# delta*u*B of every second state built tokens first and turned by TensorE into PSUM for the scan of a selective state-space layer

## The chip, the cores and the metric

The kernel runs on one core of one Trainium2 chip. Its time is the device time of one execution in microseconds. Five engines work side by side, each through its own instruction queue in order: TensorE (PE, with its weight loads PEld), VectorE (DVE), ScalarE (ACT), GpSimd (POOL) and SyncE (SP, which here only issues DMAs). SBUF is the working memory with 128 partitions; PSUM is the memory that TensorE writes into.

## What is computed

An image batch x of shape (4, 128, 128, 128), rows, columns, channels last, goes through two residual layers, each on a group-normalised input:

```
x = x + deformable_conv(group_norm(x))       # layer 0: offsets, bilinear samples, depthwise 3x3, pointwise
x = x + mamba2(group_norm(x))                # layer 1: every image row is a sequence of 128 tokens
```

Layer 1 is two blocks, one after the other, of this form (256 inner channels d, 16 states n, all fp32):

```
u, res = split(h @ in_w);  u = silu(causal_conv4(u) + cb)
dt, Bm, Cm = split(u @ xw);  delta = softplus(dt @ dtw + dtb);  A = -exp(A_log)
for t in tokens:                             # per channel d and state n
    s[d,n] = exp(delta[t,d]*A[d,n]) * s[d,n] + delta[t,d]*u[t,d]*Bm[t,n]
    y[t,d] = sum_n s[d,n] * Cm[t,n]
h = ((y + u*D) * silu(res)) @ out_w
```

## The kernel before

Layer 1 works on groups of `SR` = 4 image rows, so on `TB` = 512 tokens; the 256 channels are `NC` = 2 halves of 128 partitions. A job is one group in one of the two blocks (`NL` = 2): 4 images x 32 groups x 2 = 256 jobs. Their order is group 0 block 0, group 1 block 0, group 0 block 1, group 1 block 1, then the next pair of groups. `layer1` calls `pre` of the next job and then `main` of this one.

`pre` (L484) makes what the scan needs: four-tap convolution by 4 matmuls per channel half into a PSUM tile `pu`, Silu on ACT (L508), the gate `g` (`pr`, L513 to L518), the projection `pdb` and its copy `dbl` (L521, L524), B and C sent to DRAM as `bcd` (L526), then `pdt` and the softplus for each half: Abs, Exp, plus one, Ln on ACT (L538 to L546), two VectorE instructions for each half (L547, L548), and `de` (delta) and `du` (delta times u) for both halves (L549, L550). A job of block 0 starts from a load of layer 0's result; a job of block 1 needs the output of the same group in block 0.

`main` (L553) opens a PSUM tile `y` of two banks with u*D (L561) and then runs 8 steps q, each with `NQ` = 2 states. A step loads the rows of B and of C for its states from `bcd`, broadcast to all partitions (L570); ACT clears the first token of each row in `da` (L575, so that a scan starts anew there) and writes exp(delta*A) into the rest (L580, one instruction per half and state); VectorE multiplies `du` by B into `hs` for each state (L586), scans all 2048 numbers per partition in one instruction (L592), and multiplies the result by C (L596); TensorE transposes the 16 pieces of 128 x 128 and adds them up in `y` (L604, shown under the helper's line L128), which sums over the states and turns to tokens first. Behind the last step VectorE multiplies `y` by the gate (L607), TensorE turns the product back (`pyg`, L612), ACT copies it (`yg`, L613), TensorE applies the output projection (`pout`, L617 or L624 and L626) and ACT copies the result out (L619 or L630).

Layer 0 of image 0 runs alone. Then layer 0 of image b+1 is interleaved with layer 1 of image b, and layer 1 of the last image runs alone. Layer 0 works in units: GpSimd issues 8 gathers for a unit (L364), VectorE weighs the samples (`gw`, L382, two products of 1024), TensorE transposes and adds them into `p4` (helper line L128), ACT copies `p4` out (L396), and TensorE sums the 3 x 3 convolution into `acc` (L415).

The instructions are written in program order; a scheduler then sets the order on each engine, and tiles of one pool and tag take turns in its `bufs` buffers: a new tile waits until the last reader of the tile that had its buffer is done. The PSUM buffers of 512 fp32 numbers per partition are shared out like this: pool `ps`, tag "t", 2 (all of layer 0 but `acc`), `psa` 2 (`acc`), `ps1`, tag "t", 2 (`pu`, `pr`, `pdb`, `pdt`, `pyg`, `pout`), `psy` 2 (`y`).

Of the kernel before, what the change touches and what calls it, by code (L numbers as in the profile page):

```python
# [17 lines left out]
P = 128  # L18
# [45 lines left out]
def block_kernel(ctx: ExitStack, tc: tile.TileContext, a: dict, out: bass.AP):  # L64
# [24 lines left out]
    cw = ctx.enter_context(tc.tile_pool(name="w", bufs=1))  # L89
    small = ctx.enter_context(tc.tile_pool(name="small", bufs=1))  # L90
    pb = ctx.enter_context(tc.tile_pool(name="l0b", bufs=1))
    ps = ctx.enter_context(tc.tile_pool(name="l0ps", bufs=2, space=PSUM))
    psa = ctx.enter_context(tc.tile_pool(name="l0psa", bufs=2, space=PSUM))
    p2 = ctx.enter_context(tc.tile_pool(name="l1p2", bufs=1))
    pd = ctx.enter_context(tc.tile_pool(name="l1d", bufs=3, space=DRAM))
    ps1 = ctx.enter_context(tc.tile_pool(name="l1ps", bufs=2, space=PSUM))
    psy = ctx.enter_context(tc.tile_pool(name="l1psy", bufs=1, space=PSUM))

    def loadw(name, shape, src=None, pool=cw, tag=None):
# [33 lines left out]


    dw = loadw("dw", [P, NT, NT], pool=p2, tag="dbl")
    dwb = loadw("dwb", [P, NT], pool=p2, tag="ot")
    pw = loadw("pw", [P, NT, CG], pool=p2, tag="u")
    pwb = loadw("pwb", [P, 1], pool=p2, tag="w1")
    nc.vector.tensor_tensor(
# [15 lines left out]
    alog = loadw("alog", [P, NL, NC, NS], pool=p2, tag="dbl")  # L155
    nc.scalar.activation(aneg, alog, AF.Exp)
    nc.vector.tensor_scalar(aneg, aneg, -1.0, None, ALU.mult)
    dpar = loadw("dpar", [P, NL, NC], pool=p2, tag="ot")
# [4 lines left out]
    cvw = loadw("cvw", [P, NL, DCONV, NC * P], pool=p2, tag="hs")  # L163
    for l in range(NL):
        nc.vector.tensor_tensor(
            inc[:, l], cvw[:, l], inw[:, l].unsqueeze(1).to_broadcast([P, DCONV, NC * P]), ALU.mult
        )


# [312 lines left out]
    def pre(st, l):  # L484

        blk = st["blk"]
        nm = f"{blk}_{l}"
        if l == 0:
            x1t = load_x1(blk, nm)
            st["h"] = next_h()  # L490
            scale, bias = gn2[blk * SR // H]
            nc.scalar.activation(
                st["h"][:, :, DCONV - 1 :], x1t.rearrange("p (s t) -> p s t", s=SR),
                AF.Identity, scale=scale, bias=bias,
            )
        h = st["h"]
        u = p2.tile([P, NC, TB], F32, tag="u", name=f"u_{nm}")
        for c in range(NC):
            px = ps1.tile([P, TB], F32, tag="t", name=f"pu_{nm}_{c}")
            for j in range(DCONV):  # L500
                nc.tensor.matmul(  # L501
                    px.rearrange("p (s t) -> p s t", s=SR),
                    inc[:, l, j, c * P : (c + 1) * P],
                    h[:, :, j : j + P],
                    start=(j == 0),
                    stop=(j == DCONV - 1),
                )
            nc.scalar.activation(u[:, c], px, AF.Silu, bias=cvb[:, l, c : c + 1])  # L508
        g = p2.tile([P, SR, NC * P], F32, tag="g", name=f"g_{nm}", bufs=2)
        for i in range(SR // 2):  # L510
            px = ps1.tile([P, 2, NC * P], F32, tag="t", name=f"pr_{nm}_{i}")
            for j in range(2):
                nc.tensor.matmul(  # L513
                    px[:, j], h[:, 2 * i + j, DCONV - 1 :], resw[:, l, :],
                    start=(j == 0), stop=True, skip_group_check=True,
                )

            tc.keep_in_program_order(nc.scalar.activation(g[:, 2 * i : 2 * i + 2], px, AF.Silu))  # L518
        pdb = ps1.tile([P, TB], F32, tag="t", name=f"pdb_{nm}")
        for c in range(NC):  # L520
            nc.tensor.matmul(pdb[0:XP], xpw[:, l, c, :], u[:, c], start=(c == 0), stop=(c == NC - 1))  # L521

        dbl = p2.tile([XP, TB], F32, tag="dbl", name=f"dbl_{nm}")
        nc.scalar.activation(dbl, pdb[0:XP], AF.Identity, bias=xpb)  # L524
        bcd = pd.tile([2 * NS, TB], F32, tag="bcd", name=f"bcd_{nm}")
        nc.sync.dma_start(bcd, dbl[DTR + 1 : XP, :])  # L526


        de = p2.tile([P, NC, TB], F32, tag="de", name=f"de_{nm}", bufs=2)
        du = p2.tile([P, NC, TB], F32, tag="du", name=f"du_{nm}", bufs=2)  # L530
        es, pdts = [], []
        for c in range(NC):
            pdt = ps1.tile([P, TB], F32, tag="t", name=f"pdt_{nm}_{c}")
            nc.tensor.matmul(
                pdt, dtw[:, l, c * P : (c + 1) * P], dbl[0 : DTR + 1, :], start=True, stop=True
            )
            e = p2.tile([P, TB], F32, tag="e", name=f"e_{nm}_{c}", bufs=2)
            nc.scalar.activation(e, pdt, AF.Abs)  # L538
            nc.scalar.activation(e, e, AF.Exp, scale=-1.0)
            es.append(e)  # L540
            pdts.append(pdt)
        for c in range(NC):
            e = es[c]
            w1 = p2.tile([P, TB], F32, tag="w1", name=f"w1_{nm}_{c}")
            nc.scalar.activation(w1, e, AF.Identity, bias=1.0)
            nc.scalar.activation(du[:, c], w1, AF.Ln)  # L546
# [3 lines left out]
        nc.vector.tensor_tensor(du, de, u, ALU.mult)  # L550
        st.update(u=u, g=g, delta=de, du=du, bcd=bcd)

    def main(st, l):  # L553

        blk = st["blk"]
        nm = f"{blk}_{l}"

        y = psy.tile([P, SR, NC, P], F32, tag="y", name=f"y_{nm}")
        for i in range(SR):
            for c in range(NC):  # L560
                nc.tensor.matmul(  # L561
                    y[:, i, c], st["u"][:, c, i * P : (i + 1) * P], ddiag[:, l, c, :],
                    start=(i % 2 == 0 and c == 0), stop=False, skip_group_check=True,
                )
        for q in range(NS // NQ):
            bc = []
            for w in range(2):
                t = p2.tile([P, NQ, TB], F32, tag=f"bc{w}", name=f"bc{w}_{nm}_{q}", bufs=2)
                n0 = w * NS + q * NQ
                nc.sync.dma_start(t, st["bcd"][n0 : n0 + NQ, :].partition_broadcast(P))  # L570
                bc.append(t)
            da = das[n_da[0] % NDA]
            n_da[0] += 1

            nc.scalar.copy(da.rearrange("p c n s t -> p (c n s) t")[:, :, 0], zero)  # L575
            for c in range(NC):
                dv = st["delta"][:, c].rearrange("p (s t) -> p s t", s=SR)
                for n in range(NQ):
                    s = q * NQ + n
                    nc.scalar.activation(  # L580
                        da[:, c, n, :, 1:], dv[:, :, 1:], AF.Exp, scale=aneg[:, l, c, s : s + 1]
                    )
            hs = p2.tile([P, NC, NQ, TB], F32, tag="hs", name=f"hs_{nm}_{q}")

            for n in range(NQ):
                nc.vector.scalar_tensor_tensor(  # L586
                    hs[:, :, n, :], st["du"], ones[:, 0:1],
                    bc[0][:, n].unsqueeze(1).to_broadcast([P, NC, TB]),
                    op0=ALU.mult, op1=ALU.mult,
                )  # L590
            df = da.rearrange("p c n s t -> p (c n s t)")
            nc.vector.tensor_tensor_scan(  # L592
                df, df, hs.rearrange("p c n t -> p (c n t)"), zero[:, 0:1], ALU.mult, ALU.add
            )
            dc = da.rearrange("p c n s t -> p c (n s t)")
            nc.vector.scalar_tensor_tensor(  # L596
                dc, dc, ones[:, 0:1],
                bc[1].rearrange("p n t -> p (n t)").unsqueeze(1).to_broadcast([P, NC, NQ * TB]),
                op0=ALU.mult, op1=ALU.mult,
            )  # L600
            for c in range(NC):
                for n in range(NQ):
# [145 lines left out]
```

## Time and profile before

| | |
|---|---|
| median of 3 runs | 26672.16 us (26664.46 to 26679.19) |
| the profiled execution | 26698.06 us, of which its span 26696.0 us |
| layer 0 of image 0 alone | 0 to about 3400 us |
| layer 1 of images 0 to 2 beside layer 0 of images 1 to 3 | about 3400 to 21356 us |
| layer 1 of image 3 alone | about 21356 us to the end |

Busy time of the engines in two of these stages, in us and as a share:

| stretch | PE | DVE | ACT | POOL | granted PE clock |
|---|---|---|---|---|---|
| 3400 to 21350 us | 14338 (80%) | 17483 (97%) | 8669 (48%) | 13634 (76%) | 0.89 |
| 21350 us to the end | 2794 (52%) | 5065 (95%) | 2695 (50%) | 0 | 0.69 |

In the lines that follow, a group is a source line, its engine and operation, output<-inputs, their shapes and the count, then the busy time and the mean of one instruction in ns, then the idle time of the engine just before and what ended it. In a timeline a row is the start in us, the duration in us of the row's instructions, engine, line and operation. The strings of 40 digits give a share in tenths for each fortieth of the span.

### The profile page before, as it was taken

The page shows a single profiled execution, that of the slowest core. Times are in us where ns is not written, and L with a number is a line of the kernel's source. Part 1 is how long each engine was busy: PE and PEld are TensorE (multiplying, and loading weights), DVE is VectorE, ACT ScalarE, POOL GpSimd, SP SyncE. Part 2 cuts the span into 40 slices and gives each one's busy share as a digit, 9 for nine tenths or more (in the row PEclk, how much of TensorE's full clock was granted, in tenths as well). Part 3 has the DMA queues.
Part 4 walks back from the last instruction along what each step waited for, and adds up shares of the span by engine and source line. Part 5 has one row for each costly group of instructions (what it writes and reads, how often), then busy time and mean ns, then how long its engine had stood idle before and what let it go on. Part 6 is the DMA issues. An engine that isn't in the chain of part 4 may idle for free. (4 is left out here: it accounts for less than half of the span.)

```text
span 26696.0 us, 294801 instructions
## 1 busy us (share of the span) xinstructions
PE 19620.5 (73%) x112196; PEld 13523.4 (51%) x112196; DVE 23505.8 (88%) x14042; ACT 11605.1 (43%) x18181; POOL 16017.0 (60%) x9222
## 2 busy tenths in 40 slices
PE   4777788878888778887888778888888655555555
PEld 3444455555555555555555555555555443434344
DVE  2232289999999999999999999999999999999999
ACT  0000044444444544444444454444445455555554
POOL 4777777878877767888878667877878400000000
PEclk7888888888999888888998888899998866666666
DMA  5363344456544444455544444444444333333332
GB/s 146 114 172 107 106 147 155 157 170 183 165 153 154 149 144 155 158 173 181 164 154 153 148 143 151 156 150 152 154 154 156 130 107 106 107 106 107 107 106 102
DMA packets 1994602, 3804.53 MB, mean 143 GB/s; under 512 B 771796, under 2 KB 1116116, under 8 KB 1993053
## 3 DMA queue, kind: packets, MB, share of 16 engines
q1 hardware_dynamic: 1550812, 2577.13, 29.9%
q0 software_dynamic: 442368, 1208.55, 14.4%
q8 instruction: 880, 14.42, 0.2%
q14 instruction: 542, 4.43, 0.0%
HBM read 3567.63 MB, written 217.05 MB: 142 GB/s over the span
## 5 line engine op out<-in xcount | busy, mean ns | idle before, releaser
L364 POOL DMA_INDIRECT gt<-table,idx x9216 | 16016.3, 1738 | 5031.5 <-issue 2999.5
L592 DVE TENSOR_TENSOR_SCAN da<-da,zero,hs 128x2048 f32<-128x2048 f32 x2048 | 9176.1, 4481 | 351.7 <-ACT da L580 247.1
L128 PE MATMUL y<-ident,da 128*128 128x128 f32 x32768 | 5252.0, 326 | 3956.1 <-DVE da L596 3955.4
L580 ACT ACTIVATE da<-de,aneg 128x508 f32<-128x508 f32 x8192 | 5550.5, 712 | 5605.2 <-PE y L128 5351.0
L128 PEld LDWEIGHTS y<-ident,da 128*128 128x128 f32 x32768 | 4682.4, 171 | 4953.3 <-DVE da L596 2520.6
L415 PE MATMUL acc<-s,wc 128*64 128x256 f32 (+3 forms) x38400 | 6403.2, 453 | 761.4 <-ACT s L396 760.9
L586 DVE SCALAR_TENSOR_TENSOR hs<-du,ones,bc 128x1024 f32<-128x1024 f32 x4096 | 5093.2, 1277 | 0.0
L415 PEld LDWEIGHTS acc<-s,wc 128*64 128x64 f32 x38400 | 3352.0, 145 | 3083.2 <-issue 1446.2
L596 DVE SCALAR_TENSOR_TENSOR da<-da,ones,bc 128x2048 f32<-128x2048 f32 x2048 | 4807.9, 2348 | 25.9
L382 DVE TENSOR_TENSOR gw<-gt,wt 128x1024 f32<-128x1024 f32 x2304 | 2786.4, 1213 | 2133.3 <-DMA gt<-table,idx 1500.9
L128 PE MATMUL p<-ident,gw 128*128 128x128 f32 x18432 | 2724.3, 299 | 1714.1 <-DVE gw L382 1706.7
L128 PEld LDWEIGHTS p<-ident,gw 128*128 128x128 f32 x18432 | 2292.8, 154 | 2329.3 <-DVE gw L382 1752.7
L396 ACT COPY s<-p 128x512 f32<-128x512 f32 x1152 | 668.6, 581 | 3989.8 <-PE p L128 3982.0
L501 PE MATMUL pu<-hp,inc 128*128 128x512 f32 x4096 | 1808.3, 593 | 0.0
L580 ACT ACT_TABLE_LOAD x1016 | 1303.5, 1283 | 16.8 <-PE y L128 5.7
L501 PEld LDWEIGHTS pu<-hp,inc 128*128 128x128 f32 x4096 | 751.2, 188 | 865.9 <-issue 865.2
L508 ACT ACTIVATE u<-pu,w_cvb 128x512 f32<-128x512 f32 x512 | 324.6, 684 | 1468.9 <-PE y L561 1461.4
L561 PEld LDWEIGHTS y<-ddiag,u 128*128 128x128 f32 x4096 | 579.5, 200 | 192.0 <-issue 192.0
L612 PE MATMUL pyg<-ident,g 128*128 128x128 f32 x2048 | 353.9, 328 | 425.7 <-DVE g L607 424.8
L546 ACT ACT_TABLE_LOAD x500 | 641.5, 1283 | 8.9
L561 PE MATMUL y<-ddiag,u 128*128 128x128 f32 x4096 | 612.1, 284 | 0.0
L263 PE MATMUL pof<-xn,w_offw 128*64 128x512 f32 x2304 | 585.0, 613 | 20.0 <-ACT xn L257 12.0
(118 smaller groups left out, 11036.3 us busy)
## 6 DMA issues: line engine op xcount, KB each, us to landing
bc<-bcd SPq DMA_DIRECT2D x4096, 512.0 KB
gt<-table,idx POOLq DMA_INDIRECT x9216
table<-xt SPq DMA_DIRECT2D x984, 128.0 KB
xt<-in_x SPq DMA_DIRECT2D x124, 320.0 KB
xr<-in_x SPq DMA_DIRECT2D x128, 256.0 KB
x<-xo SPq DMA_DIRECT2D x128, 256.0 KB
x1t<-x SPq DMA_DIRECT2D x128, 256.0 KB
x1t_o<-x SPq DMA_DIRECT2D x128, 256.0 KB
```

The costliest lines, as they stand in the source:

```text
L128: nc.tensor.matmul(o, v, ident, is_transpose=True, start=start, stop=stop, skip_group_check=True)
L364: nc.gpsimd.indirect_dma_start(out=gt[:, v, r], out_offset=None, in_=flat, in_offset=bass.IndirectOffsetOnAxis(ap=idx[:, ri, o : o + 1], a ...
L382: nc.vector.tensor_tensor(gw.rearrange("p r s v c -> p (r s) v c"), gts[h].rearrange("p v r (s c) -> p (r s) v c", c=CG), wv.unsqueeze(3). ...
L396: nc.scalar.copy(st[:, :, 1 : W + 1], p4)
L415: nc.tensor.matmul(accs[b, j + i0][CG * g : CG * g + CG, q : q + rb - ra, :], wc[sl, v, e, :], st[p + 4 * g if p < 4 else 8][sl, ra:rb, kx ...
L501: nc.tensor.matmul(px.rearrange("p (s t) -> p s t", s=SR), inc[:, l, j, c * P : (c + 1) * P], h[:, :, j : j + P], start=(j == 0), stop=(j ...
L546: nc.scalar.activation(du[:, c], w1, AF.Ln)
L561: nc.tensor.matmul(y[:, i, c], st["u"][:, c, i * P : (i + 1) * P], ddiag[:, l, c, :], start=(i % 2 == 0 and c == 0), stop=False, skip_grou ...
L580: nc.scalar.activation(da[:, c, n, :, 1:], dv[:, :, 1:], AF.Exp, scale=aneg[:, l, c, s : s + 1])
L586: nc.vector.scalar_tensor_tensor(hs[:, :, n, :], st["du"], ones[:, 0:1], bc[0][:, n].unsqueeze(1).to_broadcast([P, NC, TB]), op0=ALU.mult, ...
L592: nc.vector.tensor_tensor_scan(df, df, hs.rearrange("p c n t -> p (c n t)"), zero[:, 0:1], ALU.mult, ALU.add)
L596: nc.vector.scalar_tensor_tensor(dc, dc, ones[:, 0:1], bc[1].rearrange("p n t -> p (n t)").unsqueeze(1).to_broadcast([P, NC, NQ * TB]), op ...
```

## The change

In every step q the first state goes on as before: VectorE multiplies `du` by a broadcast row of B, but GpSimd does so in the last image. The product of the second state is made tokens first: at the start of `main`, `du` is transposed by TensorE in two pieces (`pdu`) and copied by ACT into `dut`; in each step ACT scales the four rows' pieces of `dut` by a column of B (`bt`, which `pre` now makes by transposing `dbl`), and 8 transposes turn the result into two PSUM tiles `px`, which the scan reads as its second operand. The scan of 2048 becomes one of 1024 for the first state and two of 512 for the second; it writes to `hs` and not over `da`, whose first column of each row is cleared once at the start. The product with C is one instruction per state. Of B one row is broadcast per step and not two. To make room in PSUM, tag "t" of `ps` and of `ps1` have one buffer each, and `psx` has two.

```diff
-    ps = ctx.enter_context(tc.tile_pool(name="l0ps", bufs=2, space=PSUM))
+    ps = ctx.enter_context(tc.tile_pool(name="l0ps", bufs=1, space=PSUM))
...
-    ps1 = ctx.enter_context(tc.tile_pool(name="l1ps", bufs=2, space=PSUM))
+    ps1 = ctx.enter_context(tc.tile_pool(name="l1ps", bufs=1, space=PSUM))
+    psx = ctx.enter_context(tc.tile_pool(name="l1psx", bufs=2, space=PSUM))
...
-    NDA = 3
-    das = [cw.tile([P, NC, NQ, SR, P], F32, name=f"da{i}") for i in range(NDA)]
-    zero = cw.tile([P, NC * NQ * SR], F32, name="zero")
-    nc.vector.memset(zero, 0.0)
+    NDA = 4
+    das = [cw.tile([P, NC, SR, P], F32, name=f"da{i}") for i in range(NDA)]
+    for t in das:
+        nc.vector.memset(t, 0.0)
...
+        pbt = ps1.tile([P, SR, XP], F32, tag="t", name=f"pbt_{nm}")
+        for i in range(SR):
+            nc.tensor.transpose(pbt[:, i, :], dbl[:, i * P : (i + 1) * P], ident[0:XP, 0:XP])
+        bt = p2.tile([P, SR, NS], F32, tag="bt", name=f"bt_{nm}", bufs=2)
+        nc.scalar.copy(bt, pbt[:, :, DTR + 1 : DTR + 1 + NS])
...
+        dut = p2.tile([P, SR, NC * P], F32, tag="dut", name=f"dut_{nm}")
+        for k in range(SR // 2):
+            pt = ps1.tile([P, 2, NC, P], F32, tag="t", name=f"pdu_{nm}_{k}")
+            for i in range(2):
+                for c in range(NC):
+                    o = (2 * k + i) * P
+                    nc.tensor.transpose(pt[:, i, c, :], st["du"][:, c, o : o + P], ident)
+            nc.scalar.copy(dut[:, 2 * k : 2 * k + 2], pt.rearrange("p s c d -> p s (c d)"))
         for q in range(NS // NQ):
-            bc = []
-            for w in range(2):
...
-            nc.scalar.copy(da.rearrange("p c n s t -> p (c n s) t")[:, :, 0], zero)
...
+            bs = p2.tile([P, TB], F32, tag="bs", name=f"bs_{nm}_{q}", bufs=2)
+            nc.sync.dma_start(bs, st["bcd"][q * NQ : q * NQ + 1, :].partition_broadcast(P))
+            cs = p2.tile([P, NQ, TB], F32, tag="cs", name=f"cs_{nm}_{q}", bufs=2)
+            nc.sync.dma_start(cs, st["bcd"][NS + q * NQ : NS + q * NQ + NQ, :].partition_broadcast(P))
+            hs = [p2.tile([P, NC, TB], F32, tag="hs", name=f"hs_{nm}_{q}_{n}", bufs=4) for n in range(NQ)]
...
+            bv = bs.unsqueeze(1).to_broadcast([P, NC, TB])
+            if last:
+                nc.gpsimd.tensor_tensor(hs[0], st["du"], bv, ALU.mult)
+            else:
+                nc.vector.scalar_tensor_tensor(hs[0], st["du"], ones[:, 0:1], bv, op0=ALU.mult, op1=ALU.mult)
+            h0 = hs[0].rearrange("p c t -> p (c t)")
+            nc.vector.tensor_tensor_scan(
+                h0, da[0].rearrange("p c s t -> p (c s t)"), h0, 0.0, ALU.mult, ALU.add
+            )
+            s = q * NQ + 1
+            xs = [p2.tile([P, 2, NC * P], F32, tag="xs", name=f"xs_{nm}_{q}_{k}", bufs=2) for k in range(SR // 2)]
+            for i in range(SR):
+                nc.scalar.activation(xs[i // 2][:, i % 2], dut[:, i], AF.Copy, scale=st["bt"][:, i, s : s + 1])
             for c in range(NC):
...
+                px = psx.tile([P, SR, P], F32, tag="x", name=f"px_{nm}_{q}_{c}")
+                for i in range(SR):
+                    nc.tensor.transpose(px[:, i, :], xs[i // 2][:, i % 2, c * P : (c + 1) * P], ident)
+                nc.vector.tensor_tensor_scan(
+                    hs[1][:, c], da[1][:, c].rearrange("p s t -> p (s t)"), px.rearrange("p s t -> p (s t)"),
+                    0.0, ALU.mult, ALU.add,
+                )
             for n in range(NQ):
                 nc.vector.scalar_tensor_tensor(
-                    hs[:, :, n, :], st["du"], ones[:, 0:1],
-                    bc[0][:, n].unsqueeze(1).to_broadcast([P, NC, TB]),
+                    hs[n], hs[n], ones[:, 0:1], cs[:, n].unsqueeze(1).to_broadcast([P, NC, TB]),
                     op0=ALU.mult, op1=ALU.mult,
                 )
-            df = da.rearrange("p c n s t -> p (c n s t)")
-            nc.vector.tensor_tensor_scan(
-                df, df, hs.rearrange("p c n t -> p (c n t)"), zero[:, 0:1], ALU.mult, ALU.add
-            )
...
```

The rest of the diff moves set-up tiles to other tags (the convolution weights come in two loads and not one) and lets the transposes into `y` read `hs`.

More of the change, by code (lines that the diff above doesn't have):

```diff
@@ L135, in block_kernel @@
     dw = loadw("dw", [P, NT, NT], pool=p2, tag="dbl")
-    dwb = loadw("dwb", [P, NT], pool=p2, tag="ot")
+    dwb = loadw("dwb", [P, NT], pool=p2, tag="yg")
     pw = loadw("pw", [P, NT, CG], pool=p2, tag="u")
@@ L157, in block_kernel @@
     nc.vector.tensor_scalar(aneg, aneg, -1.0, None, ALU.mult)
-    dpar = loadw("dpar", [P, NL, NC], pool=p2, tag="ot")
+    dpar = loadw("dpar", [P, NL, NC], pool=p2, tag="u")
     for l in range(NL):
@@ L162, in block_kernel @@
     inw = loadw("inw", [P, NL, NC * P], a["inw"][:, :, 0 : NC * P], pool=p2, tag="yg")
-    cvw = loadw("cvw", [P, NL, DCONV, NC * P], pool=p2, tag="hs")
     for l in range(NL):
+        cvw = p2.tile([P, DCONV, NC * P], F32, tag="hs", name=f"w_cvw_{l}", bufs=4)
+        nc.sync.dma_start(cvw, a["cvw"][:, l])
         nc.vector.tensor_tensor(
-            inc[:, l], cvw[:, l], inw[:, l].unsqueeze(1).to_broadcast([P, DCONV, NC * P]), ALU.mult
+            inc[:, l], cvw, inw[:, l].unsqueeze(1).to_broadcast([P, DCONV, NC * P]), ALU.mult
         )
@@ L550, in pre @@
         nc.vector.tensor_tensor(du, de, u, ALU.mult)
-        st.update(u=u, g=g, delta=de, du=du, bcd=bcd)
+        pbt = ps1.tile([P, SR, XP], F32, tag="t", name=f"pbt_{nm}")
[3 more added lines that the diff above has]
+        nc.scalar.copy(bt, pbt[:, :, DTR + 1 : DTR + 1 + NS])
+        st.update(u=u, g=g, delta=de, du=du, bcd=bcd, bt=bt)
     def main(st, l):
         blk = st["blk"]
+        last = blk * SR // H == B - 1
         nm = f"{blk}_{l}"
@@ L564, in main @@
                 )
-        for q in range(NS // NQ):
-            bc = []
-            for w in range(2):
[L568 to L573, printed above, removed]
-            nc.scalar.copy(da.rearrange("p c n s t -> p (c n s) t")[:, :, 0], zero)
-            for c in range(NC):
[L577 to L581, printed above, removed]
-                    )
-            hs = p2.tile([P, NC, NQ, TB], F32, tag="hs", name=f"hs_{nm}_{q}")
+        dut = p2.tile([P, SR, NC * P], F32, tag="dut", name=f"dut_{nm}")
@@ new lines, in main @@
+        for k in range(SR // 2):
[5 more added lines that the diff above has]
+            nc.scalar.copy(dut[:, 2 * k : 2 * k + 2], pt.rearrange("p s c d -> p s (c d)"))
+        for q in range(NS // NQ):
+            bs = p2.tile([P, TB], F32, tag="bs", name=f"bs_{nm}_{q}", bufs=2)
[3 more added lines that the diff above has]
+            hs = [p2.tile([P, NC, TB], F32, tag="hs", name=f"hs_{nm}_{q}_{n}", bufs=4) for n in range(NQ)]
+            da = []
+            for n in range(NQ):
+                d = das[n_da[0] % NDA]
+                n_da[0] += 1
+                s = q * NQ + n
+                for c in range(NC):
+                    dv = st["delta"][:, c].rearrange("p (s t) -> p s t", s=SR)
+                    nc.scalar.activation(d[:, c, :, 1:], dv[:, :, 1:], AF.Exp, scale=aneg[:, l, c, s : s + 1])
+                da.append(d)
+            bv = bs.unsqueeze(1).to_broadcast([P, NC, TB])
[11 more added lines that the diff above has]
+                nc.scalar.activation(xs[i // 2][:, i % 2], dut[:, i], AF.Copy, scale=st["bt"][:, i, s : s + 1])
+            for c in range(NC):
+                px = psx.tile([P, SR, P], F32, tag="x", name=f"px_{nm}_{q}_{c}")
[5 more added lines that the diff above has]
+                )
@@ L585, in main @@
             for n in range(NQ):
                 nc.vector.scalar_tensor_tensor(
-                    hs[:, :, n, :], st["du"], ones[:, 0:1],
-                    bc[0][:, n].unsqueeze(1).to_broadcast([P, NC, TB]),
+                    hs[n], hs[n], ones[:, 0:1], cs[:, n].unsqueeze(1).to_broadcast([P, NC, TB]),
                     op0=ALU.mult, op1=ALU.mult,
                 )
-            df = da.rearrange("p c n s t -> p (c n s t)")
-            nc.vector.tensor_tensor_scan(
-                df, df, hs.rearrange("p c n t -> p (c n t)"), zero[:, 0:1], ALU.mult, ALU.add
-            )
@@ L595, in main @@
[L595 to L602, printed above, removed]
+                for c in range(NC):
                     for i in range(SR):
-                        add_transposed(y[:, i, c], da[:, c, n, i, :], False, q == NS // NQ - 1 and n == NQ - 1)
+                        add_transposed(
+                            y[:, i, c], hs[n][:, c, i * P : (i + 1) * P], False,
+                            q == NS // NQ - 1 and n == NQ - 1,
+                        )
@@ L628, in main @@
                     )
-            ot = p2.tile([P, SR, P], F32, tag="ot", name=f"ot_{nm}")
+            ot = p2.tile([P, SR, P], F32, tag="w1", name=f"ot_{nm}")
             nc.scalar.copy(ot.rearrange("p r c -> p (r c)"), po)
```

## The prediction

> **What bounds the kernel now.** I read the page's engine shares and 40 slices first, then the costliest groups, then busy time by stretch, then the timeline of one period and of one block boundary in the last image.
>
> ```profile
> span 26696.0 us, 294801 instructions
> PE 19620.5 (73%) x112196; PEld 13523.4 (51%) x112196; DVE 23505.8 (88%) x14042; ACT 11605.1 (43%) x18181; POOL 16017.0 (60%) x9222
> DVE  2232289999999999999999999999999999999999
> PEclk7888888888999888888998888899998866666666
> ```
> VectorE is full from the sixth slice on; only the first stage (layer 0 of image 0 alone, to 3400 us) leaves it room. A second less of its work is a second less of time, so long as its queue never stops.
>
> ```profile
> L592 DVE TENSOR_TENSOR_SCAN da<-da,zero,hs 128x2048 f32<-128x2048 f32 x2048 | 9176.1, 4481 | 351.7 <-ACT da L580 247.1
> L586 DVE SCALAR_TENSOR_TENSOR hs<-du,ones,bc 128x1024 f32<-128x1024 f32 x4096 | 5093.2, 1277 | 0.0
> L596 DVE SCALAR_TENSOR_TENSOR da<-da,ones,bc 128x2048 f32<-128x2048 f32 x2048 | 4807.9, 2348 | 25.9
> ```
> One step q is two of L586, one L592, one L596: 2 x 1.277 + 4.481 + 2.348 = 9.383 us. Next, one period of the last image and the boundary behind it (start, duration):
>
> ```profile
> 23008.29 2.48 DVE L586 SCALAR_TENSOR_TENSOR hs<-du,ones,bc 128x1024 f32<-128x1024 f32 x2
> 23010.90 4.48 DVE L592 TENSOR_TENSOR_SCAN da<-da,zero,hs 128x2048 f32<-128x2048 f32 x1
> 23015.42 2.35 DVE L596 SCALAR_TENSOR_TENSOR da<-da,ones,bc 128x2048 f32<-128x2048 f32 x1
> 23017.69 2.48 DVE L586 SCALAR_TENSOR_TENSOR hs<-du,ones,bc 128x1024 f32<-128x1024 f32 x2
> ...
> 23032.17 7.03 PE L501 MATMUL pu<-hp,inc 128*128 128x512 f32 x16
> 23042.46 1.89 PE L513 MATMUL pr<-w_resw,hp 128*128 128x256 f32 x8
> 23048.18 1.91 PE L521 MATMUL pdb<-u,w_xpw 128*41 128x512 f32 x4
> 23050.87 1.98 PE L534 MATMUL pdt<-dbl,w_dtw 9*128 9x512 f32 x4
> 23054.82 1.28 ACT L546 ACT_TABLE_LOAD   x1
> 23069.03 1.20 DVE L550 TENSOR_TENSOR du<-de,u 128x1024 f32<-128x1024 f32 x1
> ```
> The period is 9.40 us, the sum of the durations: nothing is between. `pre` of a later job runs from pu (23032) to du (23069) while VectorE goes on with steps of `main`, which need nothing from it. So a chain of over 35 us at every one of the 256 boundaries is hidden today. By the L607 rows image 0's blocks start near 3400 and the last image's near 21356: a block (8 steps) lasts 17956/192 = 93.5 us beside layer 0 and (26696 - 21356)/64 = 83.4 us in the last image.
>
> **The change, part by part.**
>
> VectorE's work. The scan is cut into one of 1024 from SBUF and two of 512 whose second operand lies in PSUM. L586 and L596 give 1.046 ns per element and 0.206 us fixed; a scan that keeps such a fixed part takes 2.35 us for 1024 and 1.28 us for 512 (2.24 and 1.12 if all of it scaled). PSUM as source: L548 reads it and takes 0.682, L547 the same size from SBUF 0.678, so nothing. No row has a scan with one SBUF input; the far lower bound is L548's rate, 0.68. I take 1.28, since two SBUF inputs do not halve L586's rate, so the slow pace is the scan's own. The C product becomes two of 1.277. A step costs 1.277 + 2.35 + 2 x 1.28 + 2 x 1.277 = 8.74 us, and 7.46 in the last image, where the B product goes to GpSimd. Gain: 0.64 x 8 = 5.1 us per block, 15.4 in the last image.
>
> Added in a step, beside VectorE: ACT gets 4 scaled copies of 256, 0.41 (L243, 260 elements) to 0.48 us (on the line from L343's 0.366 for 128 to L580's 0.712 for 508); I take 0.5. With four L580 it has 4 x 0.71 + 4 x 0.50 = 4.9 us of 7.46. PE gets 8 transposes; 16 of them took 3.65 us in the slow clock of the last image, so 24 take 5.5 us of 7.46. The built program puts step q's copies and transposes ahead of step q-1's products, so inside a block both stay hidden. The L575 copies go, and the broadcasts fall from four rows to three: both off the path. SP's queue issues these loads one step ahead, as before, and POOL's queue holds nothing but the product in the last image. Set-up edits happen once.
>
> GpSimd's product has no row: between VectorE's product of 1.21 us (L549) and GpSimd's own dearest group, 1.74 us (L364), it fits in a 7.46 us step. If it held up VectorE for its whole length it would cost up to 512 x 1.74 = 0.89 ms. L586 takes 1.277 us while GpSimd gathers and 1.279 in the last image without, so I take 0 and keep 0.89 as the other end.
> [...]
>
> The boundary. Both tag-"t" pools fall from two banks to one, and the new transposes of du (pdu) and of dbl (pbt) use the bank of `pre`. The built program's PE order at a boundary of the last image, buffer numbers cut:
>
> ```
> pyg_126_0  y(ddiag)  pout_126_0  pu_126_1_0  pu_126_1_1  pr  pr  pdb_126_1
> pdt_126_1_0  pdt_126_1_1  pbt_126_1  pdu_127_0_0  pdu_127_0_1  px_127_0_0
> ```
> So job 127_0's first px, which VectorE's first PSUM scan waits for, stands behind the whole `pre` of 126_1, and this behind 126_0's output. What is queued behind that scan on VectorE: all the rest of the block. ACT's order is the same, and with one bank each product waits for the copy-out of the last. The chain C from the end of L607 (g):
> - pyg, yg: 1.15 (24110.10 to 24111.25) + 0.59, now twice in a row, then pout 3.62 (24112.29, L617) and its copy 0.59, hand-overs 0.1 each: 7.9.
> - pu: half of 7.03 + Silu 0.68 + 0.1, twice: 8.6. pr: half of 1.89 + 0.60 + 0.1, twice: 3.3. pdb 1.91 + dbl 0.68 + 0.1: 2.7.
> - first pdt 1.15 to its Abs (23050.87 to 23052.02), Abs 0.60, table 1.28, Exp 0.62, L545 0.62, then L547 + L548 on VectorE, 1.36, before the bank is free: 5.7. Before, both pdt stood side by side. Second: 4.3 to L545, then 1.4 on VectorE and 0.7 for pbt: 6.4. bt: 0.3 (between L575's 0.21 and L343's 0.37).
> - pdu 1.15, dut 0.59, two scaled copies 1.0, dut 0.59, two copies 1.0, px 0.5 and hand-overs: 5.0.
> C = 7.9 + 8.6 + 3.3 + 2.7 + 5.7 + 6.4 + 0.3 + 5.0 = 39.9, say 40 us; beside layer 0 ACT also copies two s tiles (0.58 each) and VectorE one statistics group (0.69) inside it: 42.
>
> A block, from g to g, is C, then what VectorE still has to do: two PSUM scans 2.56, C product 1.28, seven steps, the next block's head, g 1.21. Last image: 2.56 + 1.28 + 7 x 7.46 + 2.35 + 1.21 = 59.6, + 40 = 99.6 us, 16.2 more than 83.4. Beside layer 0: 2.56 + 1.28 + 7 x 8.74 + 1.28 + 1.21 = 67.5; layer 0 has 93.5 - 75.1 - 6.35 (L547 to L550, L607) = 12 us of VectorE per block, of which the built order puts seven or eight products of 1.21 inside the chain, so 2 remain: 67.5 + 2 + 42 = 111.5, 18.0 more than 93.5.
> The first stage, with one bank for p, loses nothing to 0.2 ms (a 0.58 us copy for each of 288 units of 11.8 us); I take 0.
> **Sum**: 26.70 + 192 x 0.0180 + 64 x 0.0162 = 26.70 + 3.46 + 1.04 = **31.2 ms**. The profiled run took 26698 us, 26 over the median of 26672; that is nothing here.
>
> **Rivals.**
> 1. *The chain is hidden after all, and the gain stays*: 192 x 5.1 + 64 x 15.4 = 1.96 ms, 24.7 ms, faster. For it: before, `pre` was hidden. It decides where C falls below what a block saves and covers: the added 4.50 ms over 256 blocks is 17.6 us, so C under 24. The rows that are ACT's and VectorE's alone (17 us) and pu (7.03) reach that without any other matmul. 5%, of which 1 near no change.
> 2. *GpSimd's product blocks VectorE* in the last image: up to 31.2 + 0.89 = 32.1 ms. [...] 23%.
> 3. *The chain is longer*: PE goes cold in its gaps (the page grants 0.6 in the last image) and pu, pr, pdb, pdt double, +12.8 us; half of that, 6.4 x 256 = 1.6 ms, gives 32.8. For it: gaps of several us at pdt; against it: pu ran at full pace behind pout. 14%.
> 4. *The chain is shorter*: warm transposes and pout and hand-overs at nothing take off 5 us, 1.3 ms: 29.9; faster PSUM scans would go the same way, and both together reach 29. 8%.
>
> **How the numbers follow.** The likeliest has 50%, its own range 30.4 to 32.0 (C by 3 us). The range 29.5 to 32.9 takes in rivals 2 to 4 nearly whole. Under 0.2% (53 us) would not be told from no change: 1%, faster 4%, slower 95%.
>
> **What would show it.** VectorE idle some 20 us per block beside layer 0 and 30 us in the last image, waiting for px; its busy time near 21.5 ms; scans of 2.35 and 1.28; exp and ln tables loaded twice each per block. Wrong would be: no idle time before the first px scan of a block, or a chain from g to it under 24 us.

## The result and the profile after

The changed kernel takes 31183.35 us (median of 4 runs, 31163.41 to 31192.35), beside 26675.67 us for the kernel before in the same comparison: 1.169 times as long, interval 1.167 to 1.171. The forecast was 31200 us, slower. The profiled execution took 31184.21 us, its span 31182.4.

First the page of the kernel after, its engine shares and VectorE's 40 slices, and then groups (busy us, mean ns of one | idle us just before, and what ended it):

```profile
PE 23808.8 (76%) x131652; PEld 16026.7 (51%) x131652; DVE 20847.6 (67%) x17629; ACT 14695.9 (47%) x24611; POOL 12320.8 (40%) x9734
...
DVE  2322577777777777777777777777777766666666
...
L384 DVE TENSOR_TENSOR gw<-gt,wt 128x1024 f32<-128x1024 f32 x2304 | 2782.9, 1220 | 4376.1 <-PE p L129 2421.8
...
L620 DVE TENSOR_TENSOR_SCAN hs<-da,px 128x512 f32<-128x512 f32 x4096 | 4841.4, 1201 | 703.4 <-PE px L619 703.4
L625 DVE SCALAR_TENSOR_TENSOR hs<-hs,ones,cs 128x1024 f32<-128x1024 f32 x4096 | 5097.1, 1279 | 0.2
L608 DVE TENSOR_TENSOR_SCAN hs<-da,hs 128x1024 f32<-128x1024 f32 x2048 | 4659.4, 2275 | 1.0
...
L604 POOL TENSOR_TENSOR hs<-du,bs 128x1024 f32<-128x1024 f32 x512 | 1821.1, 3557 | 4668.6 <-PE y L129 4273.2
...
L549 DVE SCALAR_TENSOR_TENSOR e<-w,e 128x512 f32<-128x512 f32 x512 | 356.6, 696 | 4408.8 <-ACT w L547 4408.7
```
VectorE has 2.7 ms less work than before (20.85 against 23.51 ms), and yet it was 88% busy and is 67%. It waits before the softplus (L549, 4.4 ms) and before layer 0's products (L384, 4.4 ms, of which 2.05 ms come ahead of the first g, where the kernel before has 1.99), and hardly before the scan out of PSUM (L620, 0.7 ms). The group that carries the idle time is only the first in VectorE's queue behind the gap; what is late has to be looked for in the timeline. One boundary of the last image, of the kernel after (start, duration; in brackets the idle time before and what ended it):

```profile
28043.53 1.23 DVE L637 TENSOR_TENSOR g<-y,g 128x1024 f32<-128x1024 f32 x1 [0.37 <-PE y L129]
28044.67 1.72 DVE L625 SCALAR_TENSOR_TENSOR hs<-hs,ones,cs 128x1024 f32<-128x1024 f32 x1
...
28052.48 3.70 PE L503 MATMUL pu<-hp,inc 128*128 128x512 f32 x8
28057.03 3.70 PE L503 MATMUL pu<-hp,inc 128*128 128x512 f32 x8 [0.63 <-ACT u L510]
28065.15 1.91 PE L523 MATMUL pdb<-u,w_xpw 128*41 128x512 f32 x4 [0.69 <-ACT g L520]
28067.83 1.12 PE L536 MATMUL pdt<-dbl,w_dtw 9*128 9x512 f32 x2 [0.77 <-ACT dbl L526]
28072.22 0.69 DVE L549 SCALAR_TENSOR_TENSOR e<-w,e 128x512 f32<-128x512 f32 x1 [25.82 <-ACT w L547]
28073.69 2.07 PE L536 MATMUL pdt<-dbl,w_dtw 9*128 9x512 f32 x2 [4.74 <-DVE de L550]
28079.03 0.69 DVE L549 SCALAR_TENSOR_TENSOR e<-w,e 128x512 f32<-128x512 f32 x1 [5.39 <-ACT w L547]
28081.45 1.11 PE L582 MATMUL pdu<-ident,du 128*128 128x128 f32 x4 [0.30 <-ACT bt L558]
28084.15 1.06 PE L619 MATMUL px<-ident,xs 128*128 128x128 f32 x4
28086.51 2.33 DVE L620 TENSOR_TENSOR_SCAN hs<-da,px 128x512 f32<-128x512 f32 x2 [3.06 <-PE px L619]
```
g ends at 28044.76, the scan out of PSUM starts at 28086.51: 41.75 us. Between them lie this block's output (7.7 us up to pu), the whole `pre` of the next job, one product behind the other through one bank, then du's transposes, and only then px. The first wait in VectorE's queue, 25.82 us, is booked to L549, because the scheduler put `pre`'s two softplus instructions ahead of the scan. The second, 5.39 us, is the second pdt, which had to wait for the bank; the third, 3.06 us, is px itself.

From the starts of L637 (L607 before) in the two timelines, the period of a block:

| | before | after | difference | times blocks |
|---|---|---|---|---|
| start of the first g | 3570.1 | 3555.8 | -14.3 us | |
| beside layer 0, us per block | 93.12 | 112.69 | +19.57 | x 191 = +3.74 ms |
| last image, us per block | 83.28 | 95.11 | +11.83 | x 64 = +0.76 ms |

The sum is 4.48 ms of the 4.51 ms lost. A block lost 19.6 us beside layer 0, where 18.0 were forecast, and 11.8 in the last image, where 16.2 were.

### The profile page after: what moved, and what is told of

The parts are those of the page before. It is cut to its first block, busy times and chain, and to the rows that moved or that the text cites. A ratio compares the mean times of both kernels' runs of the same rounds, so it can differ in the third digit from the quotient of the medians.

```text
span 31182.4 us, 348664 instructions
## 1 busy us (share of the span) xinstructions
PE 23808.8 (76%) x131652; PEld 16026.7 (51%) x131652; DVE 20847.6 (67%) x17629; ACT 14695.9 (47%) x24611; POOL 12320.8 (40%) x9734
## 4 chain that ended last, share of the span: by engine, by line
DVE 29%; issue 28%; PE 23%; POOL 13%; ACT 4%; DMA 2%; SPq 0%; DVEq 0%; POOLq 0%; ACTq 0%
POOL gt L366 13%; DVE hs L608 9%; DVE hs L620 8%; DVE hs L625 6%; PE acc L417 6%; PE pu L503 4%; DVE hs L606 3%; PE p L129 2%; DMA gt<-table,idx 2%; PE y L129 2%; PE pdt L536 1%; PE pr L515 1%; PE y L571 1%; PE pdb L523 1%; PE px L619 1%
## 5 line engine op out<-in xcount | busy, mean ns | idle before, releaser
L366 POOL DMA_INDIRECT gt<-table,idx x9216 | 10499.0, 1139 | 14166.6 <-DVE gw L384 11167.8
L598 ACT ACTIVATE da<-de,aneg 128x508 f32<-128x508 f32 x8192 | 5455.6, 711 | 6460.0 <-DVE hs L608 3723.5
L129 PE MATMUL y<-ident,hs 128*128 128x128 f32 x32768 | 5821.8, 345 | 1595.3 <-DVE hs L625 1538.8
L129 PEld LDWEIGHTS y<-ident,hs 128*128 128x128 f32 x32768 | 5054.0, 181 | 2655.0 <-DVE hs L625 2299.9
L384 DVE TENSOR_TENSOR gw<-gt,wt 128x1024 f32<-128x1024 f32 x2304 | 2782.9, 1220 | 4376.1 <-PE p L129 2421.8
L619 PE MATMUL px<-ident,xs 128*128 128x128 f32 x16384 | 3167.2, 325 | 3060.4 <-DVE hs L620 2992.4
L620 DVE TENSOR_TENSOR_SCAN hs<-da,px 128x512 f32<-128x512 f32 x4096 | 4841.4, 1201 | 703.4 <-PE px L619 703.4
L625 DVE SCALAR_TENSOR_TENSOR hs<-hs,ones,cs 128x1024 f32<-128x1024 f32 x4096 | 5097.1, 1279 | 0.2
L608 DVE TENSOR_TENSOR_SCAN hs<-da,hs 128x1024 f32<-128x1024 f32 x2048 | 4659.4, 2275 | 1.0
L619 PEld LDWEIGHTS px<-ident,xs 128*128 128x128 f32 x16384 | 2096.6, 163 | 4390.0 <-DVE hs L620 2438.7
L615 ACT ACTIVATE xs<-dut,bt 128x256 f32<-128x256 f32 x8192 | 3501.7, 496 | 183.7 <-PE px L619 151.2
L549 DVE SCALAR_TENSOR_TENSOR e<-w,e 128x512 f32<-128x512 f32 x512 | 356.6, 696 | 4408.8 <-ACT w L547 4408.7
L606 DVE SCALAR_TENSOR_TENSOR hs<-du,ones,bs 128x1024 f32<-128x1024 f32 x1536 | 1958.6, 1275 | 0.0
L510 ACT ACTIVATE u<-pu,w_cvb 128x512 f32<-128x512 f32 x512 | 352.2, 688 | 1390.9 <-PE pu L503 1388.2
```

Source lines behind the costliest of these rows:

```text
L366: nc.gpsimd.indirect_dma_start(out=gt[:, v, r], out_offset=None, in_=flat, in_offset=bass.IndirectOffsetOnAxis(ap=idx[:, ri, o : o + 1], a ...
L384: nc.vector.tensor_tensor(gw.rearrange("p r s v c -> p (r s) v c"), gts[h].rearrange("p v r (s c) -> p (r s) v c", c=CG), wv.unsqueeze(3). ...
L598: nc.scalar.activation(d[:, c, :, 1:], dv[:, :, 1:], AF.Exp, scale=aneg[:, l, c, s : s + 1])
L606: nc.vector.scalar_tensor_tensor(hs[0], st["du"], ones[:, 0:1], bv, op0=ALU.mult, op1=ALU.mult)
L608: nc.vector.tensor_tensor_scan(h0, da[0].rearrange("p c s t -> p (c s t)"), h0, 0.0, ALU.mult, ALU.add)
L615: nc.scalar.activation(xs[i // 2][:, i % 2], dut[:, i], AF.Copy, scale=st["bt"][:, i, s : s + 1])
```

## The experiments

None of these kernels leaves out a part of the computation. Ratios are to the kernel before in the same comparison (26699 us for the first four, 26687 for the next four, 27341 for the last two).

**One: pdu in the pool psx, which holds px, and nothing else changed.**
```diff
-            pt = ps1.tile([P, 2, NC, P], F32, tag="t", name=f"pdu_{nm}_{k}")
+            pt = psx.tile([P, 2, NC, P], F32, tag="x", name=f"pdu_{nm}_{k}")
```


> The changed kernel with one line altered: the transposes of du (pdu) take their two PSUM tiles from the pool of px (free at a block's start), not from the single bank that pre uses. Everything else stays: one bank each for pre and layer 0, the same instructions, the same lengths. Theory (the loss is the wait of a block's first px behind the whole pre of the next job): the wait at the head of every block goes; a step costs VectorE 7.99 us beside layer 0 and 6.80 in the last image as measured in the changed kernel, so a block is 8 x 7.99 + 6.35 + 11.2 = 81.5 and 8 x 6.80 + 6.35 = 60.8 us, and the time 3.4 + 192 x 0.0815 + 64 x 0.0608 = 22.9 ms, up to 25 if TensorE, busy 91 us of a block beside layer 0, bounds instead: faster than before. Rival (single PSUM banks themselves, or the added ACT and PE work, cost the time): within 3% of 31.2 ms.

Measured: 27070.4 us, ratio 1.0139 (1.0122 to 1.0156). Another pool for two tiles takes back 4.1 of the 4.5 ms. From g to the first scan out of PSUM it is now 5.2 us on the mean of 20 blocks beside layer 0 (10000 to 12000 us), and nothing in the last image. So the wait is what the prediction called C. The size was missed: the expected 22.9 to 25 ms left VectorE no idle time, and it has some. Its waits between 6000 and 12000 us (total us, times, longest), 62 blocks:

```profile
DVE hs L620 <- PE px L619: 432.1, 90, 19.1
DVE e L549 <- ACT w L547: 233.5, 49, 15.9
DVE gw L384 <- PE p L129: 77.6, 22, 9.6
```
7.0 and 3.8 us per block at px and at the softplus: a block takes 96.9 us. In the last image (78.1 us) px costs 8.3 us per block, and GpSimd gets in the way, as the sixth and eighth experiments show. And ACT, now free to go from `pre` to the steps and back, loads its tables more often: 2392 times at 1.283 us against 1554 in the changed kernel and 2036 in the one before; in the last image that is 12.8 us of ACT per block (653 us over 51 blocks). That these loads cost VectorE anything is not shown: the kernel of experiment two makes 2934 of them and the fastest of all, eight, 2770.

**Two: the kernel before with one bank each in ps and ps1.**
```diff
-    ps = ctx.enter_context(tc.tile_pool(name="l0ps", bufs=2, space=PSUM))
+    ps = ctx.enter_context(tc.tile_pool(name="l0ps", bufs=1, space=PSUM))
...
-    ps1 = ctx.enter_context(tc.tile_pool(name="l1ps", bufs=2, space=PSUM))
+    ps1 = ctx.enter_context(tc.tile_pool(name="l1ps", bufs=1, space=PSUM))
```


> The kernel before with nothing but the two pools cut to one PSUM bank each (layer 0's p and the like, pre's pu, pdt and the like). main takes nothing from pre's bank there until its end. Theory: the longer chain of pre stays hidden behind eight steps of 9.4 us; 26.7 to 27.1 ms. Rival (one bank each is the loss by itself): 29 ms or more.

Measured: 26555.43 us, ratio 0.9946 (0.9927 to 0.9966). One bank makes `pre` longer (from the start of pu to the end of du 38.7 us before and 53.2 now in the last image, 42.6 and 53.0 beside layer 0), but as long as nothing of this job stands behind it, that costs nothing. It even gains 0.5%, all of it in the last image (81.2 us per block against 83.3; 93.2 against 93.1 beside layer 0); why was not looked into.

**Three: the first state's product on VectorE in the last image too.**
```diff
-        last = blk * SR // H == B - 1
+        last = False
```


> The changed kernel with the last image's product of du and B on VectorE instead of GpSimd, as in the other images. Theory (GpSimd's product hardly holds VectorE up): a step of the last image goes from 6.80 to 7.99 us less some 0.09 us that VectorE's two-input instructions lose beside GpSimd now, +0.55 ms: 31.7 ms. Rival (GpSimd's product blocks VectorE for a good part of its 3.56 us): no slower, 30.6 to 31.2 ms.

Measured: 31799.17 us, ratio 1.1911 (1.1887 to 1.1934), so 0.62 ms slower than the changed kernel: the last image's block goes from 95.1 to 105.0 us; a step grows from 6.80 to 7.99, so its 8 steps are 9.5 of the 9.9 us. As the changed kernel stands, GpSimd's product is worth its place.

**Four: the second pdt in psx.**
```diff
-            pdt = ps1.tile([P, TB], F32, tag="t", name=f"pdt_{nm}_{c}")
+            pdt = (psx.tile([P, TB], F32, tag="x", name=f"pdt_{nm}_{c}") if c else ps1.tile([P, TB], F32, tag="t", name=f"pdt_{nm}_{c}"))
```


> The changed kernel with only the second pdt of pre in a bank of px's pool, so that both pdt stand side by side again; pdu stays behind pre. Theory (a block's time follows the chain from g to the first px one for one): the chain loses a table load pair or so and the second pdt's wait, 4 to 6 us of some 41 to 45; 256 x 5 us = 1.3 ms less: 29.9 ms (29.6 to 30.2), with the head's wait still there. Rival (the chain is not what sets the block): within 0.3 ms of 31.2 ms.

Measured: 30208.46 us, ratio 1.1315 (1.1292 to 1.1337), 0.98 ms faster than the changed kernel. In the last image C falls from 40.8 to 35.7 us (means of 15 and 17 blocks of 27000 to 28500 us) and the block from 95.1 to 90.05. There a link taken out of the chain comes off the block one for one. Beside layer 0 it is less: 5.8 us off C (44.9 to 39.1, 10000 to 12000 us), 3.4 off the block (112.7 to 109.25).

**Five: one and four together.**
```diff
-            pdt = ps1.tile([P, TB], F32, tag="t", name=f"pdt_{nm}_{c}")
+            pdt = (psx.tile([P, TB], F32, tag="x", name=f"pdt_{nm}_{c}") if c else ps1.tile([P, TB], F32, tag="t", name=f"pdt_{nm}_{c}"))
...
-            pt = ps1.tile([P, 2, NC, P], F32, tag="t", name=f"pdu_{nm}_{k}")
+            pt = psx.tile([P, 2, NC, P], F32, tag="x", name=f"pdu_{nm}_{k}")
```


> e1 and e4 together: pdu and the second pdt both in px's pool. Beside layer 0 e1's VectorE still waits 3.8 us per block for the softplus of the next job and 6.7 us for px. Theory (these are what is left of the longer chain of pre, now inside a block): the first wait goes, 26.4 to 26.8 ms. Rival (in e1 the chain is hidden and TensorE's load beside layer 0 is what is left): within 0.2 ms of 27.07 ms.

Measured: 30060.91 us, ratio 1.1262 (1.124 to 1.1285). Both expectations missed, by some 3 ms: the two edits each made the kernel faster, but the second undoes the gain of the first, and the time is near that of experiment four alone. C is back at 34.0 us in the last image and 38.0 beside layer 0 (10000 to 12000 us). One boundary of this kernel:

```profile
26001.47 1.23 DVE L637 TENSOR_TENSOR g<-y,g 128x1024 f32<-128x1024 f32 x1 [0.37 <-PE y L129]
...
26025.05 1.98 PE L536 MATMUL pdt<-dbl,w_dtw 9*128 9x512 f32 x4 [0.77 <-ACT dbl L526]
...
26026.96 1.12 PE L582 MATMUL pdu<-ident,du 128*128 128x128 f32 x4
...
26029.78 0.69 DVE L549 SCALAR_TENSOR_TENSOR e<-w,e 128x512 f32<-128x512 f32 x1 [25.45 <-ACT w L547]
```
pdu now stands behind the next job's second pdt in psx as it stood behind its pbt in ps1. The wait goes with the order of the tiles in a pool, whichever pool that is.

**Six: one, with the product on VectorE.** Against the kernel of experiment one:
```diff
-            if last:
+            if False:
                 nc.gpsimd.tensor_tensor(hs[0], st["du"], bv, ALU.mult)
```


> e1 with the last image's product of du and B on VectorE instead of GpSimd. In e1's last image VectorE's instructions with two SBUF inputs are longer than beside layer 0 (L608 2.79 against 2.28, L625 1.43 against 1.28, L551 2.26 and L552 1.72 against 1.21). Theory (GpSimd's product holds VectorE up there, because it now starts before VectorE's scan or C product): taking it away gives back 8 x 0.51 + 16 x 0.15 + 1.6 = 8.1 us per block and costs 8 x 1.2 = 9.6; the time stays within 0.15 ms of 27.07 ms, and the four durations fall to 2.28, 1.28, 1.21 and 1.21. Rival (the product on GpSimd is free, the longer durations have another cause): +0.6 ms as in e3, 27.7 ms, with the durations still long.

Measured: 26785.58 us, ratio 1.0035 (1.0022 to 1.0049): 0.28 ms faster than experiment one, where no change was expected. The last image's block falls from 78.1 to 74.1 us although VectorE has 8 products more in it. Of experiment one, two pairs in which GpSimd starts first, and of the kernel after, one in which VectorE does:

```profile
24112.35 2.35 POOL L604 TENSOR_TENSOR hs<-du,bs 128x1024 f32<-128x1024 f32 x1 [4.99 <-DVE hs L620]
24113.31 3.53 DVE L608 TENSOR_TENSOR_SCAN hs<-da,hs 128x1024 f32<-128x1024 f32 x1
...
24131.19 1.28 DVE L625 SCALAR_TENSOR_TENSOR hs<-hs,ones,cs 128x1024 f32<-128x1024 f32 x1
24131.35 3.34 POOL L604 TENSOR_TENSOR hs<-du,bs 128x1024 f32<-128x1024 f32 x1 [5.06 <-PE y L129]
24132.39 4.45 DVE L608 TENSOR_TENSOR_SCAN hs<-da,hs 128x1024 f32<-128x1024 f32 x1
```
```profile
28006.90 2.28 DVE L608 TENSOR_TENSOR_SCAN hs<-da,hs 128x1024 f32<-128x1024 f32 x1
28007.02 4.32 POOL L604 TENSOR_TENSOR hs<-du,bs 128x1024 f32<-128x1024 f32 x1 [2.48 <-PE y L129]
28009.10 2.31 DVE L620 TENSOR_TENSOR_SCAN hs<-da,px 128x512 f32<-128x512 f32 x2
28011.32 2.46 DVE L625 SCALAR_TENSOR_TENSOR hs<-hs,ones,cs 128x1024 f32<-128x1024 f32 x2
```
GpSimd's end plus the scan's own 2.28 us gives VectorE's end in both pairs of experiment one: 24114.70 + 2.28 = 24116.98 (24116.84 measured), 24134.69 + 2.28 = 24136.97 (24136.84). (GpSimd's 3.34 us in the second pair hold its own wait for the C product that began just ahead of it.) In the kernel after it is the other way round: the scan keeps its 2.28, ends at 28009.18, and GpSimd ends 2.16 us later, under the two PSUM scans, which keep their 1.2. In these three whoever starts later waits for the other's end. So it is in all 447 pairs of the kernel after in which the scan starts first: GpSimd ends 2.14 to 2.16 us behind it. In experiment one 127 of 142 scans that start after GpSimd end 2.1 to 2.2 us behind it; in the other 15 the scan's record starts only 0.03 us later, and the scan goes first. The prediction did not ask who starts first.

**Seven and eight: the products of the second state tokens first in the last image alone,** beside layer 0 one scan of 1024 out of SBUF for each state, pdu in psx as in experiment one; eight has the last image's first product on VectorE too. The core of seven against the changed kernel, and what eight adds:
```diff
+            nb = 1 if last else NQ
...
+            for n in range(nb):
+                bv = bs[n].unsqueeze(1).to_broadcast([P, NC, TB])
+                if last:
+                    nc.gpsimd.tensor_tensor(hs[n], st["du"], bv, ALU.mult)
+                else:
+                    nc.vector.scalar_tensor_tensor(hs[n], st["du"], ones[:, 0:1], bv, op0=ALU.mult, op1=ALU.mult)
+                h0 = hs[n].rearrange("p c t -> p (c t)")
+                nc.vector.tensor_tensor_scan(
+                    h0, da[n].rearrange("p c s t -> p (c s t)"), h0, 0.0, ALU.mult, ALU.add
+                )
+
             if last:
...
```
```diff
-                if last:
+                if False:
```


> e1 with the tokens-first product only in the last image: beside layer 0 VectorE multiplies both states' products (two rows of B) and scans each state in one instruction of 1024 from SBUF, so TensorE and ACT have nothing added there. Theory (e1's rest of the loss is the stage beside layer 0, where TensorE and ACT are loaded): a step is 2 x 1.20 + 2 x 2.18 + 2 x 1.19 = 9.14 us by start to start against 9.40 before, the block 91.4 against 93.5 us, and the last image's block 78.5 as in e1 against 83.4: 26.70 - 0.40 - 0.31 = 26.0 ms (25.8 to 26.3), faster than both kernels. Rival (one bank each or the last image carries the rest of the loss): 26.7 ms or more.

> e7 with the last image's product of the first state on VectorE too, so GpSimd does none. If GpSimd's product holds VectorE up in the last image by about what it saves, as e6 tests in e1: within 0.15 ms of e7. If it is free: e7 + 0.6 ms.

Measured: seven 26438.89 us, ratio 0.9905 (0.9888 to 0.9921); eight 26177.38 us, ratio 0.9809 (0.9793 to 0.9826). Eight is the fastest of all, 1.9% under the kernel before. Its block beside layer 0, 93.69 us, is near that of the kernel before (93.12) and not the expected 91.4; why the shorter step does not show there was not settled. The gain is in the last image, 73.98 us against 83.28. Of these 9.3 us the single bank alone gave 2.1 in experiment two. Why the turned product pays in that stage and not beside layer 0 was not taken apart; the likely reason, that ACT and TensorE have more room without layer 0, is not shown. The step from seven to eight, 78.11 to 73.98 us, is that of experiment six again; in eight no product is left on GpSimd.

**Nine and ten: pdu ahead of the next job's pre, in the one bank of ps1.** The loop over the rows' pairs moves out of `main` into a `head`; nine is the changed kernel with this, ten is kernel eight with this (and pdu back in ps1):
```diff
         for i, job in enumerate(jobs):
+            head(*job)
             if i + 1 < len(jobs):
                 pre(*jobs[i + 1])
```


> The changed kernel with the same pools and the same single bank of tag t, but with the two transposes of du written ahead of the next job's pre and not behind it. Nothing else differs. Theory (the order of the tiles in the one bank, not the number of banks, puts px behind pre): from the end of g to the first scan out of PSUM there stay the output (7.9 us by the prediction's sum) and pdu to px (5.0), so some 13 us in place of 44.9 and 40.8. The last image's block falls from 95.4 to 95.4 - 40.8 + 13 + 5.2 (pre's six VectorE instructions, which lay inside the wait before) = 72.8 us, up to 78.5 if GpSimd's product gets in the way as in the kernel with pdu in psx; beside layer 0 the block falls from 112.9 to 112.9 - 44.9 + 13 + 5.2 + 9 (layer 0's products, which lay inside the wait) = 95.2 us. Total 31.18 - 192 x 0.0177 - 64 x 0.0194 = 26.5 ms, range 26.3 to 27.2. Rival (du's transposes need a bank of their own beside pre's; with one bank for all of them the wait stays): 30.9 to 31.3 ms.

> The best kernel so far (26177 us: px in the last image alone, all products on VectorE) with pdu taken out of the pool psx and put into tag t of ps1, ahead of the next job's pre. Theory (what stands between g and the first px costs VectorE one for one, less the 3.6 us of product and scan of the first state): the 13 us of output and pdu to px leave some 9 us of idle time in each of the last image's 64 blocks, waiting for px; the block there goes from 74.0 to 83 us, the block beside layer 0 stays at 93.6, total 26.6 to 26.8 ms. Rival (a chain as short as 13 us is covered, since a wait counts only above 24 us as the prediction has it): 26.05 to 26.25 ms, no more idle time at px than now.

Measured: nine 30057.02 us, ratio 1.0995 (1.0963 to 1.1027); ten 27678.34 us, ratio 1.0125 (1.0095 to 1.0154). In this comparison the kernel before also took 2.4% longer than in the others, and the first g came at 4317 and 4296 us instead of 3527 to 3570; the blocks are therefore the better measure (ten's block beside layer 0 is that of eight). In nine C is 12.5 us in the last image, as expected (13), and 17.4 in a stretch beside layer 0, so the order of the tiles does put px behind `pre`. The block did not follow: 85.0 us and 106.2, where 72.8 to 78.5 and 95.2 were expected. VectorE's waits in nine, 25500 to 29500 us, 47 blocks:

```profile
DVE hs L626 <- PE px L625: 658.9, 141, 11.3
DVE e L549 <- ACT w L547: 201.0, 47, 4.6
```
14.0 us per block at px, three waits in each, where one of 13 less 3.6 was counted, and 4.3 at the softplus, counted at nothing: `pre` now runs among the steps, and its work on ACT and TensorE comes between a step and its px. Some 5 us more are VectorE instructions held up by GpSimd: L551 takes 3298 ns instead of 1200, L549 1679 on the mean of its two instead of 690, the scan from SBUF 2417 instead of 2285, so 2.1 + 2.0 + 8 x 0.13. Where the 11 us more than expected beside layer 0 come from was not taken apart. Ten has no product on GpSimd: 85.02 us instead of 73.98 with an expected 83, and 93.78 beside layer 0 with an expected 93.6. So a chain of some 14 us is not covered either.

## Why the prediction was right

The mechanism is the one that it named, and the total is right to 17 us in 31200. But several terms were off and cancelled, so that closeness is luck.

- **C, the chain from g to the first scan out of PSUM**: 40 forecast and 40.8 measured in the last image (15 blocks); beside layer 0 42 and 44.9 (18 blocks of 10000 to 12000 us). Term by term in the boundary above: g to pu 7.7 (7.9 forecast); pu and pr 12.7 (11.9); pdb 2.7 (2.7); first pdt 5.9 (5.7); second pdt, pbt and bt 7.8 (6.7); pdu to the scan 5.1 (5.0). What was too cheap is matmuls: each half of pu took 3.70 us (half of 7.03 forecast), each pr 1.13 (half of 1.89), and the second pdt 2.07 where the first took 1.12 (1.15 forecast for each); that is 1.7 of the 1.85 us. The second pdt came after 4.74 us without a matmul, and the granted clock, 1.00 over pu and pr, was 0.50 there. Beside layer 0 its own matmuls and ACT copies stand between these links, of which the forecast counted two ACT copies and one VectorE group. That the chain is paid for link by link in the last image was shown by experiment four.
- **The step**: forecast 8.74 and 7.46, measured 7.99 and 6.80 (period of L620 inside a block). The PSUM scan took 1.20 us, not 1.28, and the records of neighbours that do not depend on each other overlap by 0.08 to 0.1 us (in the last image 28006.90 + 2.28 against 28009.10), so the sum of durations was too long. The scan of 1024 took 2.275 (2.35 forecast) and the C product 1.279 (1.277).
- **The block**: 99.6 forecast and 95.1 measured in the last image, since seven steps were priced 0.66 us too dear each (4.6 us). Beside layer 0 111.5 and 112.7. By the 53 blocks from 6000 to 12000 us C was 3.8 us longer (45.8); outside it layer 0's work on VectorE took 4.1 us (2 forecast) and waits 2.8 (none forecast), and what is left, this layer's own instructions, 58.8 instead of 66.3, most of it the cheaper steps. The page has 2.4 ms at gw behind p. All but 0.17 ms of that comes behind the first g, where the kernel before has 0.03 ms; in those 53 blocks it is 11.8 us each, and every one of these waits lies between a g and the next scan out of PSUM. So layer 0's products, which the forecast put into the chain as work, waited in it themselves. The single bank of p by itself does not make them wait: experiment one, which has it too, shows 0.41 ms in all. 1.2 us x 192 and -4.5 us x 64 are +0.23 and -0.29 ms, which nearly cancel.
- **The first stage**, at nothing: the first g came 14 us earlier. **The copies**: xs 0.496 us against 0.5, bt 0.21 against 0.3.
- **VectorE's busy time**: 20.85 ms against near 21.5; its idle time 29.4 us per block from 6000 to 12000 us and 34.2 from 27000 to 30500, against 20 and 30. The wait was named right and looked for in the wrong place: it is booked to the softplus, not to px. Exp's and ln's tables are loaded 512 times each beside the softplus (L541, L548), twice a block as forecast.
- **The rival "hidden after all"** fell: VectorE waits from 28044 on. Its bound, C under 24 us, is too generous: experiment ten has a C of 14.3 us (17 blocks of 24000 to 25500 us, 13.0 to 15.8) and loses 11 us a block against kernel eight. The 24 us were meant as what a block may lose before it is slower than before, not as what it can hide; even so they were too many, for nine, with a C of 12.5 and 17.4 us, has longer blocks than the kernel before in both stages (85.0 against 83.3, 106.2 against 93.1).
- **The rival "GpSimd blocks VectorE"**: in the kernel after it fell, and the 0 that was taken is right to 0.05 ms: L608 takes 2.285 us in the last image against 2.271 beside layer 0, L625 1.306 against 1.270, so 512 x 0.09. It is real nonetheless: GpSimd's mean is 3.56 us, not the 1.21 to 1.74 of the bounds, and once the boundary's wait is gone a block is 4.1 us longer with it than with the product on VectorE, 0.26 to 0.28 ms in all (experiments six and eight).
- **The rival of a cold TensorE** came true in one link: in the last image the second pdt took 2.07 us in each of the 37 blocks from 27000 to 30500 us, 0.95 more than the first (granted clock 0.50 and 1.00 in the boundary above). It fell for the rest: pu takes 3.70 us for half of its 16 matmuls, 7.03 for all before, and the chain is 0.8 us longer than forecast, not 6.4. **The rival of a shorter chain** was right about the PSUM scans alone.

## What to carry over

Where a pool of PSUM banks hands out tiles in program order, a tile that this job needs must be written ahead of the next job's tiles in the same pool, or it waits for their whole chain; another pool, here one of two banks, helped only as long as nothing of that chain stood there first (experiments one and five). Written ahead it still has its own links: the 12.5 to 14 us that were left in nine and ten were paid for too. A wait shows up in the waits' list under the first instruction queued behind the gap (here the softplus), so follow the timeline to the operand that is late. Before an operation goes to GpSimd to spare VectorE, ask which of the two will start first: here, where both read two operands from SBUF, the later one waited out the other's instruction (GpSimd in all 447 pairs of the kernel after in which the scan starts first, the scan in 127 of 142 of experiment one).

## What was not expected of the hardware

- A GpSimd product of 128 x 1024 took 2.35 us when nothing held it up (2.34 to 2.36 in the 64 of the kernel after beside which VectorE did nothing), and up to 4.33 behind VectorE's scan in the kernel after; the scan took 2.28 us alone and 4.45 behind GpSimd in the second pair of experiment one above.
- A scan of 512 with one operand in PSUM took 1.20 us, on the mean 1.197 in the 767 that ran beside GpSimd's product and 1.202 in the others, and the product behind a scan of 1024 ended 2.14 to 2.16 us after it with these scans beside it, so neither was seen to lengthen the other; the scan of 1024 from SBUF took 2.275 and that of 2048 4.48, so 2.19 to 2.35 ns per element at each size.
- ACT loaded its tables 1283 ns at a time: in the last image of experiment one 255 times at da (L598), 102 at Silu (L510), 101 at Ln (L548) and 51 at the gate (L520) for 51 blocks, so five, two, two and one a block.
- The granted TensorE clock fell to 0.50 in the chain's own gaps: the second pdt, after 4.74 us without a matmul, took 2.07 us, and the first, the same two matmuls, 1.12.
